# Turning normalised features for the matmuls of a four-layer graph network: 32x32 squares and a trip through DRAM in place of 16-bit DMA transposes

## The chip, the cores and the metric

The kernel runs on one core of one Trainium2 chip. The metric is the time that the device takes for one execution, in microseconds. In the profile the engines are PE (TensorE matmul), PEld (TensorE weight load), DVE (VectorE), ACT (ScalarE), POOL (GpSimd) and SP (SyncE, which here only issues DMAs).

## What is computed

There are 32 independent graphs of 512 nodes with 256 float32 features each, and an integer adjacency matrix per graph (about 3% ones). Four attention layers follow one another; each adds its result to x:

```python
h = relu(layernorm(x))                       # ahead of each of the four layers
# layer 0: att = softmax((h A) h^T / 16 + mask); y = tanh(att (h W0 + b0)); x += tanh(att (y W1 + b1))
# layer 1: Wh = h W^T; e = leaky(src + dst^T) masked; x += softmax(e) Wh
# layer 2: Hh = h W;   e = exp(-leaky(s + d^T)) where adj, else 0; x += elu(e Hh / rowsum)
# layer 3: hl = h W; logits = hl a12 hl^T + Ax^T + Ay; att = softmax(leaky(logits) masked)
#          x += elu(h W_1 + (att h) W_2)
```

Everything is float32. Sizes are fixed: N = 512 nodes are NT = 4 tiles of P = 128, H = 256 features are HC = 2 tiles of 128.

## The kernel before

**One program, planned ahead.** The function `graph(b, ...)` lists the operations of one graph: each `op(engine, cost, after, emit, *keys)` has an engine, a cost in ns, the operations it comes after, and the tiles it uses. The class `Plan` holds all operations of the 32 graphs and of the weights' preparation. `Plan.order` is a list scheduler: each engine takes the ready operation with the earliest due time, if its buffers are free; due times are counted back from deadlines that lie some 32 to 62 us apart per graph (`APART`; the last two graphs use `APART_LAST`). Transfers with a size also queue for a wire of 200 bytes per ns. The result is one fixed order, in which the instructions are issued. Each engine, and the DMA queue of SP, then works in that order and waits where an input is late. The costs (`A_NORM, A_JOIN, V_SPLIT`, `D_TURN` and so on, in ns) thus decide the order, not the time.

**Buffers.** A pool of `PAGES` = 34 pages of 4 KB a partition holds most tiles (x, xn, hT, fa, e, hs, ...); `FLIGHT` = 6 graphs may be under way at once. `planes` (3 buffers) and `planesT` (2) serve the step that the change replaces.

**From x to hT.** `normed(l, xs)` prepares layer l: for each pair g of node tiles, DVE takes the statistics (L557, L558) and adds epsilon (L561), POOL takes the root (L564), DVE forms the offset (L567), and ACT writes the normalised, rectified features `xn` (L571), nodes on partitions. The matmuls need features on partitions, `hT` [128, 2, 512]. [...] per node tile:

1. `split` (L576) copies `xn` into two planes of 16-bit halves, on DVE, or on ACT in layer 1 (`BYACT`);
2. `turn` (L579) is one DMA transpose of the two planes, issued by SP;
3. `join` (L591), on ACT, weaves the planes together into `hT`.

Only layer 0 of graph 0 is turned by PE (`turn_pe` L584, `out_of` L587).

**What uses hT.** `block_sums` forms sums of quarters of `hT` (`hs`, L664 and L667). `seven` multiplies 2x2 blocks with seven products: `by_nodes` (L809) has 128 columns of `hT` or `hs` as the weights and 128 or 129 columns streaming, `features_t` (L783) has a weight matrix as the weights and `hT` streaming, and the scores of layers 0 and 3 (L874, L1040) have both sides from features. `attend` (L758) has a 128x128 block of the attention matrix `e` as the weights and streams the values `v` (257 to 259 columns). `again` (L918) and `second_conv` (L936) are the second half of layer 0. In each case a slice of 128 neighbouring columns, node tile t, is loaded as the weights, for instance

```python
nc.tensor.matmul(T[key][:, : LEAD + H + 1 - lead], e(l, c)[:, t * P : (t + 1) * P],
                 T[f"v{l}"][:, c, lead:], start=(c == 0), stop=(c == NT - 1))
```

Each float32 matmul of the program is two matmul records, with a weight load each, in the profile. A row of scores is made in `leaky_exp_t`: for the first and last two graphs PE turns it (L715), for the others a DVE transpose of 32x32 squares (L719) and two DMAs through DRAM (L723, L728). The adjacency arrives by node tiles (`fetch_adj`, L501), becomes 16-bit codes (L519), and is turned by DMA transposes (L522). Layer 3's maxima take two more DMA transposes a graph (L1072). Outputs leave from POOL (L1154).

Of the kernel before, what the change touches and what calls it, by code (L numbers as in the profile page):

```python
# [13 lines left out]
BF16 = mybir.dt.bfloat16  # L14
U16 = mybir.dt.uint16
AF = mybir.ActivationFunctionType
# [28 lines left out]
A_HALF_BIAS = (345.0, 460.0)  # L45
A_NORM, A_JOIN, V_SPLIT = (491.0, 590.0), (620.0, 767.0), (332.0, 422.0)
D_TURN = (1310.0, 2600.0)
V_SQUARES = (180.0, 270.0)
D_OUT, D_SPREAD = (550.0, 2500.0), (550.0, 4500.0)
D_X, D_ADJ = (550.0, 5000.0), (550.0, 5000.0)  # L50
G_LOAD = (800.0, 5000.0)
# [155 lines left out]
def kernel(  # L207
# [38 lines left out]
    TURNED = 2  # L246
    BYACT = (1,)
    LEAD = 2
# [14 lines left out]
        "w": (pair, F32, "page"), "crest": ([P, 4, N], BF16, "page"),  # L263
        "hs": ([P, 4, N // 2], F32, "page"), "fs": ([P, 4, N // 2], F32, "page"),
        "code": (turned, BF16, "code"), "adj": (turned, I32, "adj"),
        "planes": ([P, 2, H], U16, "planes"), "planesT": ([P, 2 * HC, P], U16, "planesT"),
        "bank": ([P, 512], F32, "bank"), "v": (None, F32, "v"),
# [3 lines left out]
    }  # L271
    POOLS = {"page": PAGES, "v": VALUES, "code": 1, "adj": 1, "planes": 3, "planesT": 2, "bank": 8, "sT": 2,
             "slot": FLIGHT, "ahead": FLIGHT + 1}
# [201 lines left out]
    def graph(b, adj_before, x_before):  # L475
# [12 lines left out]

        def both(kind, l=""):
            return f"{kind}{l}_0", f"{kind}{l}_1"  # L490

# [8 lines left out]
        def fetch_adj(t):  # L500
            nc.sync.dma_start(out=T["adj"][:, t, :], in_=adj[b, t * P : (t + 1) * P, :])  # L501

# [4 lines left out]
        for t in range(NT):  # L507

            got_adj.append(op("D", D_ADJ, got_adj[-1:] if b else [], partial(fetch_adj, t), "adj", size=P * N * 4))
        if b == 0:  # L510
# [41 lines left out]
        def normed(l, xs):  # L552

            def stats(t):
                nc.vector.bn_stats(T[f"st{l}"][:, t, :], T["x"][:, t, :])  # L557
                nc.vector.bn_aggr(T[f"mv{l}"][:, t, :], T[f"st{l}"][:, t, :])  # L558

            def variance(g):  # L560
                nc.vector.tensor_scalar(T[f"ve{l}"][:, two(g)], T[f"mv{l}"][:, two(g), 1], EPS, None, ALU.add)  # L561

            def root(g):
                nc.gpsimd.tensor_tensor(T[f"rstd{l}"][:, two(g)], T[f"ve{l}"][:, two(g)], mhalf[:, two(g)], ALU.pow)  # L564

            def offset(g):
                nc.vector.scalar_tensor_tensor(T[f"off{l}"][:, two(g)], T[f"mv{l}"][:, two(g), 0], -1.0,  # L567
                                               T[f"rstd{l}"][:, two(g)], ALU.mult, ALU.mult)

            def norm(t):  # L570
                nc.scalar.activation(T[f"xn{l}"][:, t, :], T["x"][:, t, :], AF.Relu,  # L571
                                     bias=T[f"off{l}"][:, t : t + 1], scale=T[f"rstd{l}"][:, t : t + 1])

            def split(t):
                bits = T[f"xn{l}"][:, t, :].bitcast(U16).rearrange("p (h b) -> p b h", b=2)
                (nc.scalar.copy if l in BYACT else nc.vector.tensor_copy)(T[f"planes{l}_{t}"], bits)  # L576

            def turn(t):
                nc.sync.dma_start_transpose(out=T[f"planesT{l}_{t}"],  # L579
                                            in_=T[f"planes{l}_{t}"].rearrange("p b h -> p (b h)"))  # L580

            def turn_pe(t, key):
                for c in range(HC):
                    nc.tensor.transpose(T[key][:, c * P : (c + 1) * P], T[f"xn{l}"][:, t, c * P : (c + 1) * P], ident)  # L584

            def out_of(t, key):
                nc.vector.tensor_copy(T[f"hT{l}"][:, :, t * P : (t + 1) * P], T[key][:, : HC * P].rearrange("p (c n) -> p c n", c=HC))  # L587

            def join(t):
                bits = T[f"hT{l}"].bitcast(U16).rearrange("p c (n b) -> p b c n", b=2)  # L590
                nc.scalar.copy(bits[:, :, :, t * P : (t + 1) * P],  # L591
                               T[f"planesT{l}_{t}"].rearrange("p (b c) n -> p b c n", b=2))

            done = []
            for g in range(NT // 2):
                a, d = (op("V", V_STATS, [xs[t]], partial(stats, t), "x", "slot") for t in (2 * g, 2 * g + 1))
                if b == l == 0:
                    for n in ("w0", "att"):
                        ready[n][0]["after"].append(d)
                a = op("V", V_TINY, [a, d], partial(variance, g))  # L600
                r = op("G", G_POW, [a], partial(root, g))
                r = op("V", V_TINY, [r], partial(offset, g))
                for t in (2 * g, 2 * g + 1):
                    flat, over = f"planes{l}_{t}", f"planesT{l}_{t}"
                    a = op("A", A_NORM, [r], partial(norm, t), "x", f"xn{l}")
                    if b == l == 0:

                        key = f"bank_n{t}"
                        a = op("PE", pe(nt=2 * HC), [a], partial(turn_pe, t, key), f"xn{l}", key)
                        done.append(op("V", V_ADD, [a], partial(out_of, t, key), f"hT{l}", key))  # L610
                        continue
                    a = op("A" if l in BYACT else "V", A_JOIN if l in BYACT else V_SPLIT, [a], partial(split, t), f"xn{l}", flat)
                    a = op("D", D_TURN, [a], partial(turn, t), flat, over)
                    done.append(op("A", A_JOIN, [a], partial(join, t), over, f"hT{l}"))
            return done
# [89 lines left out]
        def leaky_exp_t(l, vs, sign):  # L705
# [8 lines left out]
            def turn(t):  # L714
                nc.tensor.transpose(T[key][:, t * P : (t + 1) * P],  # L715
                                    T[v][:, t, 0:1].to_broadcast([P, P]), ident)

            def squares():
                nc.vector.transpose(T[f"sT{l}"].rearrange("p (t j) -> p t j", t=NT), T[v][:, :, 0:32])  # L719

            def collect():
                line.append(dram.tile([N], F32, tag=f"row_{T.places['slot']['number']}", name=f"row{l}_{b}"))
                nc.sync.dma_start(out=line[0].rearrange("(t g j) -> g t j", t=NT, j=32),  # L723
                                  in_=T[f"sT{l}"][0:P:32, :].rearrange("g (t j) -> g t j", t=NT))

# [22 lines left out]
        def attend(l, es, vs, use):  # L748
# [4 lines left out]
            for ts in parts(l):  # L753
                keys = [f"bank_a{l}{t}" for t in ts]

                def product(ts, c, keys):
                    for t, key in zip(ts, keys):
                        nc.tensor.matmul(T[key][:, : LEAD + H + 1 - lead], e(l, c)[:, t * P : (t + 1) * P],  # L758
                                         T[f"v{l}"][:, c, lead:], start=(c == 0), stop=(c == NT - 1))
# [45 lines left out]
        def by_nodes(w, right, x, p, fresh):  # L805

            k = w.shape[2]
            for j in range(2):
                nc.tensor.matmul(p[:, j * k : (j + 1) * k], right(x)[:, j * P : (j + 1) * P], w[:, x - 1, :],  # L809
                                 start=fresh and j == 0, stop=True, skip_group_check=True)  # L810
# [3 lines left out]
        if b == 0:  # L814
# [12 lines left out]
            for t in range(NT):  # L827
                key = f"bank_v0{t}"

                def values(t, key):  # L830
                    for c in range(HC):
                        nc.tensor.matmul(T[key][:, :H], T["hT0"][:, c, t * P : (t + 1) * P], w0_sb()[:, c, :],
                                         start=(c == 0), stop=(c == HC - 1))
# [4 lines left out]
            for c in range(NT):  # L838
                key = f"bank_q0{c}"

                def similar(c, key):
                    for k in range(HC):
                        nc.tensor.matmul(T[key], T["hT0"][:, k, c * P : (c + 1) * P], T["fa0"][:, k, :],
                                         start=(k == 0), stop=(k == HC - 1))
# [6 lines left out]
        else:  # L851
# [20 lines left out]
            def scores0(right, left, x, p, fresh):  # L872
                for j in range(2):
                    nc.tensor.matmul(p[:, j * N // 2 : (j + 1) * N // 2], right(x)[:, j * P : (j + 1) * P], left(x),  # L874
                                     start=fresh and j == 0, stop=True, skip_group_check=True)
# [53 lines left out]
        for g in range(NT // 2):  # L929
            key = f"bank_o{g}"  # L930

            def second_conv(g, key):
                for j in range(2):
                    t = 2 * g + j
                    for k in range(HC):
                        nc.tensor.matmul(T[key][:, j * H : (j + 1) * H], T["zT"][:, k, t * P : (t + 1) * P],  # L936
                                         w1_sb[:, k, :], start=(k == 0), stop=(k == HC - 1))
# [100 lines left out]
        def scores3(x, p, fresh):  # L1038
            for j in range(2):
                nc.tensor.matmul(p[:, j * N // 2 : (j + 1) * N // 2], left(x)[:, j * P : (j + 1) * P], right(x),  # L1040
                                 start=fresh and j == 0, stop=True, skip_group_check=True)
# [159 lines left out]
```

## Time and profile before

| | before |
|---|---|
| median of 3 runs (lowest to highest) | 2353.42 us (2351.95 to 2353.51) |
| profiled execution, first to last instruction | 2353.1 us (its own time is not listed apart) |
| granted TensorE clock | 0.999 |
| records of matmuls, DVE, ACT | 12374, 6060, 3421 |
| DMA packets, moved | 429859, 178.26 MB |
| queue 1 (SP's), share of 16 DMA engines | 31.2% |
| DMA transposes: features, codes, maxima | 508, 124, 64 |

The page gives the busy time of each engine over the whole span, then groups of instructions by line, tile and shape: busy time, mean ns of one, and after the bar the idle time just before them with what ended it. Matmuls overlap, so a mean of 381 ns for one does not mean that they are 381 ns apart; the spacing is read from runs of equal matmuls in the timeline or in the chain. Bytes and packets count the DMA side of each transfer. A wait is put down to what came last.

### The profile page before, as it was taken

The page shows a single profiled execution, that of the slowest core. Times are in us where ns is not written, and L with a number is a line of the kernel's source. Part 1 is how long each engine was busy: PE and PEld are TensorE (multiplying, and loading weights), DVE is VectorE, ACT ScalarE, POOL GpSimd, SP SyncE. Part 2 cuts the span into 40 slices and gives each one's busy share as a digit, 9 for nine tenths or more (in the row PEclk, how much of TensorE's full clock was granted, in tenths as well). Part 3 has the DMA queues.
Part 4 walks back from the last instruction along what each step waited for, and adds up shares of the span by engine and source line. Part 5 has one row for each costly group of instructions (what it writes and reads, how often), then busy time and mean ns, then how long its engine had stood idle before and what let it go on. Part 6 is the DMA issues. An engine that isn't in the chain of part 4 may idle for free.

```text
span 2353.1 us, 37623 instructions
## 1 busy us (share of the span) xinstructions
PE 2328.9 (99%) x12374; PEld 1992.0 (85%) x12374; DVE 2099.7 (89%) x6060; ACT 1719.9 (73%) x3421; POOL 254.2 (11%) x316
## 2 busy tenths in 40 slices
PE   8999999999999999999999999999999999999998
PEld 5789888888888888888898888888888888888887
DVE  8788899989889898898998889989898988987998
ACT  5677778767787677786777877677776778667874
POOL 3000101111011111011110010100101000010110
PEclk9999999999999999999999999999999999999999
DMA  7431233323333332333323334233343333321221
GB/s 192 106 78 28 57 79 79 88 66 83 72 75 84 78 83 66 70 88 90 82 58 74 80 85 90 54 82 70 88 91 68 86 68 73 86 54 33 55 49 42
DMA packets 429859, 178.26 MB, mean 76 GB/s; under 512 B 384128, under 2 KB 401664, under 8 KB 429664
## 3 DMA queue, kind: packets, MB, share of 16 engines
q1 hardware_dynamic: 424288, 157.51, 31.2%
q0 software_dynamic: 5232, 18.23, 2.4%
q8 instruction: 97, 1.59, 0.3%
q14 instruction: 98, 0.80, 0.1%
q10 hardware_dynamic: 144, 0.13, 0.0%
HBM read 67.64 MB, written 16.89 MB: 36 GB/s over the span
## 4 chain that ended last, share of the span: by engine, by line
PE 94%; DVE 4%; DMA 1%; ACT 1%; issue 0%; POOL 0%; DVEq 0%; ACTq 0%
PE bank_a L758 36%; PE bank_z L918 9%; PE bank_s3p L1040 5%; PE bank_o L936 4%; PE bank_q0p L874 4%; PE bank_f3p L783 4%; PE bank_w3p L809 4%; PE bank_v0p L809 4%; PE bank_f0p L783 4%; PE bank_s3q L1040 3%; PE bank_q0q L874 3%; PE bank_v1p L809 2%; PE bank_v3p L809 2%; PE bank_v2p L809 2%; PE bank_v3q L809 2%; PE bank_v1q L809 2%
## 5 line engine op out<-in xcount | busy, mean ns | idle before, releaser
L758 PE MATMUL bank_a<-v,e 128*128 128x258 f32 (+2 forms) x4096 | 1017.7, 381 | 0.9 <-DVE e L956 0.9
L758 PEld LDWEIGHTS bank_a<-v,e 128*128 128x128 f32 x4096 | 744.1, 190 | 108.9 <-issue 18.2
L591 ACT COPY hT<-planesT 128x512 uint16<-128x512 uint16 x508 | 377.8, 769 | 93.9 <-DMA planesT<-planes 93.2
L564 POOL TENSOR_TENSOR rstd<-ve,mhalf 128x2 f32<-128x2 f32 x256 | 216.0, 863 | 1732.3 <-DVE ve L561 1599.4
L571 ACT ACTIVATE xn<-x,off,rstd 128x256 f32<-128x256 f32 x512 | 278.0, 593 | 39.8 <-DVE off L567 38.9
L918 PE MATMUL bank_z<-e,y 128*128 128x512 f32 x512 | 240.8, 593 | 0.0
L557 DVE BATCH_NORM_STATS2 st<-x 128x6 f32<-128x256 f32 x512 | 210.5, 411 | 3.8 <-DMA x<-in_x_dram 3.8
L576 DVE COPY planes<-xn 128x512 uint16<-128x512 uint16 x380 | 156.4, 420 | 17.3 <-DMA planesT<-planes 10.2
L882 ACT ACTIVATE e<-e 128x512 f32<-128x512 f32 x124 | 77.8, 629 | 121.9 <-DVE e L893 61.8
L732 ACT ACTIVATE e<-row,v 128x512 f32<-128x512 f32 x224 | 156.6, 719 | 0.8 <-DMA row<-row 0.7
L735 ACT ACTIVATE e<-e 128x512 f32<-128x512 f32 x256 | 157.1, 630 | 0.0
L918 PEld LDWEIGHTS bank_z<-e,y 128*128 128x128 f32 x512 | 92.7, 190 | 64.9 <-issue 60.5
L695 ACT COPY v<-bank_v1p 128x258 f32<-128x258 f32 x128 | 47.7, 373 | 120.0 <-PE bank_v1p L809 119.3
L936 PE MATMUL bank_o<-w_sb,zT 128*128 128x256 f32 x512 | 118.5, 379 | 0.2 <-ACT zT L922 0.2
L1047 DVE SCALAR_TENSOR_TENSOR e<-bank_s3p,v,mask 128x256 f32<-128x256 f32 x256 | 111.0, 475 | 8.4 <-PE bank_a L758 4.4
L558 DVE BATCH_NORM_AGGREGATE mv<-st 128x2 f32<-128x6 f32 x512 | 93.2, 182 | 17.5
L936 PEld LDWEIGHTS bank_o<-w_sb,zT 128*128 128x128 f32 x512 | 95.8, 190 | 12.8 <-ACT zT L922 0.6
L664 DVE TENSOR_TENSOR hs<-hT,hs 128x256 f32<-128x256 f32 x254 | 105.1, 414 | 1.1
L667 DVE TENSOR_TENSOR hs<-hT 128x512 f32<-128x512 f32 x127 | 86.6, 682 | 14.5 <-ACT hT L591 14.3
L1086 ACT ACTIVATE e<-e,zero 128x512 f32<-128x512 f32 x128 | 88.2, 721 | 12.9 <-DVE crest L1064 11.4
L885 DVE TENSOR_TENSOR e<-bank_q0p,mask 128x512 f32<-128x512 f32 x124 | 84.5, 682 | 13.8 <-PE bank_q0p L874 12.3
L1089 DVE TENSOR_TENSOR e<-e,crest 128x512 f32<-128x512 f32 x128 | 85.9, 682 | 8.3 <-ACT crest L1083 8.1
(202 smaller groups left out, 4891.3 us busy)
## 6 DMA issues: line engine op xcount, KB each, us to landing
adj<-in_adj_dram SPq DMA_DIRECT2D x128, 256.0 KB
x<-in_x_dram SPq DMA_DIRECT2D x31, 512.0 KB
out_dram<-y POOLq DMA_DIRECT2D x31, 512.0 KB, 3.6
row<-row SPq DMA_DIRECT2D x56, 256.0 KB
planesT<-planes SPq DMA_TRANSPOSE x508
codeT<-code SPq DMA_TRANSPOSE x124
crest<-crest SPq DMA_TRANSPOSE x64
row<-sT SPq DMA_DIRECT2D x56, 2.0 KB
```

What stands on the lines that cost most here:

```text
L557: nc.vector.bn_stats(T[f"st{l}"][:, t, :], T["x"][:, t, :])
L564: nc.gpsimd.tensor_tensor(T[f"rstd{l}"][:, two(g)], T[f"ve{l}"][:, two(g)], mhalf[:, two(g)], ALU.pow)
L571: nc.scalar.activation(T[f"xn{l}"][:, t, :], T["x"][:, t, :], AF.Relu, bias=T[f"off{l}"][:, t : t + 1], scale=T[f"rstd{l}"][:, t : t + 1])
L591: nc.scalar.copy(bits[:, :, :, t * P : (t + 1) * P], T[f"planesT{l}_{t}"].rearrange("p (b c) n -> p b c n", b=2))
L735: nc.scalar.activation(e(l, c), e(l, c), AF.Exp, scale=sign)
L758: nc.tensor.matmul(T[key][:, : LEAD + H + 1 - lead], e(l, c)[:, t * P : (t + 1) * P], T[f"v{l}"][:, c, lead:], start=(c == 0), stop=(c == ...
L783: nc.tensor.matmul(p[:, : N // 2], w[:, x - 1, :], right(x), start=fresh, stop=True, skip_group_check=True)
L809: nc.tensor.matmul(p[:, j * k : (j + 1) * k], right(x)[:, j * P : (j + 1) * P], w[:, x - 1, :], start=fresh and j == 0, stop=True, skip_gr ...
L874: nc.tensor.matmul(p[:, j * N // 2 : (j + 1) * N // 2], right(x)[:, j * P : (j + 1) * P], left(x), start=fresh and j == 0, stop=True, skip ...
L918: nc.tensor.matmul(T[f"bank_z{k}"], T["y0"][:, c, k * P : (k + 1) * P], e(0, c), start=(c == 0), stop=(c == NT - 1))
L936: nc.tensor.matmul(T[key][:, j * H : (j + 1) * H], T["zT"][:, k, t * P : (t + 1) * P], w1_sb[:, k, :], start=(k == 0), stop=(k == HC - 1))
L1040: nc.tensor.matmul(p[:, j * N // 2 : (j + 1) * N // 2], left(x)[:, j * P : (j + 1) * P], right(x), start=fresh and j == 0, stop=True, skip ...
```

## The change

The features are turned in pairs of node tiles. `squares(g)` is one DVE transpose of 32x32 squares from `xn` of tiles 2g and 2g+1 (512 elements a partition) into half of a page `xt`. `away(g)` stores that half, 256 KB, to a DRAM tile `sheet`; `back(c)` loads half of `hT` from the sheet, 128 partitions by 8 runs of 64 floats. Both are plain DMAs on SP, two of each a layer; both loads come after both stores. Splits, planes and joins go. The nodes of a pair end up interleaved: column 256 g + 2 p + k of `hT` is node p of tile 2g + k. So wherever a node tile is loaded as weights, the slice takes every second column of a half, by the new helper `nodes`; the adjacency's rows are fetched so that node order agrees along the other axis (two DMAs of 64 rows a tile, into every second partition); and the row of scores is laid out in pairs. The planner has new costs `V_TURN`, `D_HALF` and `D_ROWS`.

```diff
-A_NORM, A_JOIN, V_SPLIT = (491.0, 590.0), (620.0, 767.0), (332.0, 422.0)
+A_NORM, V_TURN = (491.0, 590.0), (600.0, 700.0)
+D_ROWS = (1000.0, 5000.0)
+D_HALF = (550.0, 2500.0)
...
-        "planes": ([P, 2, H], U16, "planes"), "planesT": ([P, 2 * HC, P], U16, "planesT"),
+        "xt": ([P, 2, N], F32, "page"), 
...
+        def nodes(cols, j):
+            return cols[:, j::2]
...
         def fetch_adj(t):
-            nc.sync.dma_start(out=T["adj"][:, t, :], in_=adj[b, t * P : (t + 1) * P, :])
+            for k in range(2):
+                first = t // 2 * 2 * P + k * P + t % 2 * (P // 2)
+                nc.sync.dma_start(out=T["adj"][k::2, t, :], in_=adj[b, first : first + P // 2, :])
...
-            def split(t):
-                bits = T[f"xn{l}"][:, t, :].bitcast(U16).rearrange("p (h b) -> p b h", b=2)
-                (nc.scalar.copy if l in BYACT else nc.vector.tensor_copy)(T[f"planes{l}_{t}"], bits)
-
-            def turn(t):
-                nc.sync.dma_start_transpose(out=T[f"planesT{l}_{t}"],
-                                            in_=T[f"planes{l}_{t}"].rearrange("p b h -> p (b h)"))
+            def squares(g):
+                nc.vector.transpose(
+                    T[f"xt{l}"][:, g, :].rearrange("p (q c n k) -> p k c q n", q=4, c=HC, k=2),
+                    T[f"xn{l}"][:, two(g), :].rearrange("p t (c f q) -> p t c q f", c=HC, q=4))
+
+            def away(g):
+                if not sheet:
+                    sheet.append(dram.tile([2 * P, N], F32, tag=f"sheet_{T.places['slot']['number']}", name=f"sheet{l}_{b}"))
+                nc.sync.dma_start(out=sheet[0][g * P : (g + 1) * P, :], in_=T[f"xt{l}"][:, g, :])
+
+            def back(c):
+                d = sheet[0]
+                nc.sync.dma_start(
+                    out=T[f"hT{l}"][:, c, :].rearrange("p (a r) -> p a r", a=8),
+                    in_=bass.AP(tensor=d.tensor, offset=d.offset + c * (P // 2), ap=[[P, P], [32 * N, 8], [1, P // 2]]))
...
-            def join(t):
-                bits = T[f"hT{l}"].bitcast(U16).rearrange("p c (n b) -> p b c n", b=2)
-                nc.scalar.copy(bits[:, :, :, t * P : (t + 1) * P],
-                               T[f"planesT{l}_{t}"].rearrange("p (b c) n -> p b c n", b=2))
...
-                    a = op("A" if l in BYACT else "V", A_JOIN if l in BYACT else V_SPLIT, [a], partial(split, t), f"xn{l}", flat)
-                    a = op("D", D_TURN, [a], partial(turn, t), flat, over)
-                    done.append(op("A", A_JOIN, [a], partial(join, t), over, f"hT{l}"))
+                    ns.append(a)
+                if ns:
+                    a = op("V", V_TURN, ns, partial(squares, g), f"xn{l}", f"xt{l}")
+                    a = op("D", D_HALF, [a], partial(away, g), f"xt{l}", "slot", size=P * N * 4)
+                    done.append(a)
+            if not b == l == 0:
+                done = [tuple(op("D", D_HALF, done, partial(back, c), f"hT{l}", "slot", size=P * N * 4) for c in range(HC))] * NT
...
-                        nc.tensor.matmul(T[key][:, : LEAD + H + 1 - lead], e(l, c)[:, t * P : (t + 1) * P],
+                        nc.tensor.matmul(T[key][:, : LEAD + H + 1 - lead], nodes(e(l, c)[:, half(t // 2)], t % 2),
...
-                nc.tensor.matmul(p[:, j * k : (j + 1) * k], right(x)[:, j * P : (j + 1) * P], w[:, x - 1, :],
+                nc.tensor.matmul(p[:, j * k : (j + 1) * k], nodes(right(x), j), w[:, x - 1, :],
```

The same replacement of a slice by `nodes` is made in the scores (L874, L1040), in `second_conv` (L936), in graph 0's own products, and in the output of the row turned by PE (L715).

More of the change, by code (lines that the diff above doesn't have):

```diff
@@ L14 @@
 BF16 = mybir.dt.bfloat16
-U16 = mybir.dt.uint16
 AF = mybir.ActivationFunctionType
@@ L246 @@
     TURNED = 2
-    BYACT = (1,)
     LEAD = 2
@@ L263 @@
         "w": (pair, F32, "page"), "crest": ([P, 4, N], BF16, "page"),
-        "hs": ([P, 4, N // 2], F32, "page"), "fs": ([P, 4, N // 2], F32, "page"),
+        "xt": ([P, 2, N], F32, "page"), "hs": ([P, 4, N // 2], F32, "page"), "fs": ([P, 4, N // 2], F32, "page"),
         "code": (turned, BF16, "code"), "adj": (turned, I32, "adj"),
-        "planes": ([P, 2, H], U16, "planes"), "planesT": ([P, 2 * HC, P], U16, "planesT"),
         "bank": ([P, 512], F32, "bank"), "v": (None, F32, "v"),
@@ L271 @@
     }
-    POOLS = {"page": PAGES, "v": VALUES, "code": 1, "adj": 1, "planes": 3, "planesT": 2, "bank": 8, "sT": 2,
+    POOLS = {"page": PAGES, "v": VALUES, "code": 1, "adj": 1, "bank": 8, "sT": 2,
              "slot": FLIGHT, "ahead": FLIGHT + 1}
@@ L487, in half @@
             return slice(i * N // 2, (i + 1) * N // 2)
-        def both(kind, l=""):
-            return f"{kind}{l}_0", f"{kind}{l}_1"
+        def nodes(cols, j):
+            return cols[:, j::2]
         def e(l, c):
@@ L507, in graph @@
         for t in range(NT):
-            got_adj.append(op("D", D_ADJ, got_adj[-1:] if b else [], partial(fetch_adj, t), "adj", size=P * N * 4))
+            got_adj.append(op("D", D_ROWS, got_adj[-1:] if b else [], partial(fetch_adj, t), "adj", size=P * N * 4))
         if b == 0:
@@ L572, in norm @@
                                      bias=T[f"off{l}"][:, t : t + 1], scale=T[f"rstd{l}"][:, t : t + 1])
-            def split(t):
-                bits = T[f"xn{l}"][:, t, :].bitcast(U16).rearrange("p (h b) -> p b h", b=2)
-                (nc.scalar.copy if l in BYACT else nc.vector.tensor_copy)(T[f"planes{l}_{t}"], bits)
-            def turn(t):
-                nc.sync.dma_start_transpose(out=T[f"planesT{l}_{t}"],
-                                            in_=T[f"planes{l}_{t}"].rearrange("p b h -> p (b h)"))
+            def squares(g):
[11 more added lines that the diff above has]
+                    in_=bass.AP(tensor=d.tensor, offset=d.offset + c * (P // 2), ap=[[P, P], [32 * N, 8], [1, P // 2]]))
+            sheet = []
             def turn_pe(t, key):
@@ L586, in out_of @@
             def out_of(t, key):
-                nc.vector.tensor_copy(T[f"hT{l}"][:, :, t * P : (t + 1) * P], T[key][:, : HC * P].rearrange("p (c n) -> p c n", c=HC))
-            def join(t):
-                bits = T[f"hT{l}"].bitcast(U16).rearrange("p c (n b) -> p b c n", b=2)
-                nc.scalar.copy(bits[:, :, :, t * P : (t + 1) * P],
-                               T[f"planesT{l}_{t}"].rearrange("p (b c) n -> p b c n", b=2))
+                nc.vector.tensor_copy(T[f"hT{l}"][:, :, t // 2 * 2 * P + t % 2 : (t // 2 + 1) * 2 * P : 2],
+                                      T[key][:, : HC * P].rearrange("p (c n) -> p c n", c=HC))
             done = []
@@ L602, in normed @@
                 r = op("V", V_TINY, [r], partial(offset, g))
+                ns = []
                 for t in (2 * g, 2 * g + 1):
-                    flat, over = f"planes{l}_{t}", f"planesT{l}_{t}"
                     a = op("A", A_NORM, [r], partial(norm, t), "x", f"xn{l}")
@@ L714, in turn @@
             def turn(t):
-                nc.tensor.transpose(T[key][:, t * P : (t + 1) * P],
+                nc.tensor.transpose(nodes(T[key][:, half(t // 2)], t % 2),
                                     T[v][:, t, 0:1].to_broadcast([P, P]), ident)
             def squares():
-                nc.vector.transpose(T[f"sT{l}"].rearrange("p (t j) -> p t j", t=NT), T[v][:, :, 0:32])
+                nc.vector.transpose(T[f"sT{l}"].rearrange("p (s j k) -> p s k j", s=2, k=2), T[v][:, :, 0:32].rearrange("p (s k) j -> p s k j", k=2))
             def collect():
                 line.append(dram.tile([N], F32, tag=f"row_{T.places['slot']['number']}", name=f"row{l}_{b}"))
-                nc.sync.dma_start(out=line[0].rearrange("(t g j) -> g t j", t=NT, j=32),
-                                  in_=T[f"sT{l}"][0:P:32, :].rearrange("g (t j) -> g t j", t=NT))
+                nc.sync.dma_start(out=line[0].rearrange("(s g j) -> g s j", s=2, j=64),
+                                  in_=T[f"sT{l}"][0:P:32, :].rearrange("g (s j) -> g s j", s=2))
             def spread():
@@ L831, in values @@
                     for c in range(HC):
-                        nc.tensor.matmul(T[key][:, :H], T["hT0"][:, c, t * P : (t + 1) * P], w0_sb()[:, c, :],
+                        nc.tensor.matmul(T[key][:, :H], nodes(T["hT0"][:, c, half(t // 2)], t % 2), w0_sb()[:, c, :],
                                          start=(c == 0), stop=(c == HC - 1))
@@ L842, in similar @@
                     for k in range(HC):
-                        nc.tensor.matmul(T[key], T["hT0"][:, k, c * P : (c + 1) * P], T["fa0"][:, k, :],
+                        nc.tensor.matmul(T[key], nodes(T["hT0"][:, k, half(c // 2)], c % 2), T["fa0"][:, k, :],
                                          start=(k == 0), stop=(k == HC - 1))
@@ L873, in scores0 @@
                 for j in range(2):
-                    nc.tensor.matmul(p[:, j * N // 2 : (j + 1) * N // 2], right(x)[:, j * P : (j + 1) * P], left(x),
+                    nc.tensor.matmul(p[:, j * N // 2 : (j + 1) * N // 2], nodes(right(x), j), left(x),
                                      start=fresh and j == 0, stop=True, skip_group_check=True)
@@ L935, in second_conv @@
                     for k in range(HC):
-                        nc.tensor.matmul(T[key][:, j * H : (j + 1) * H], T["zT"][:, k, t * P : (t + 1) * P],
+                        nc.tensor.matmul(T[key][:, j * H : (j + 1) * H], nodes(T["zT"][:, k, half(t // 2)], t % 2),
                                          w1_sb[:, k, :], start=(k == 0), stop=(k == HC - 1))
@@ L1039, in scores3 @@
             for j in range(2):
-                nc.tensor.matmul(p[:, j * N // 2 : (j + 1) * N // 2], left(x)[:, j * P : (j + 1) * P], right(x),
+                nc.tensor.matmul(p[:, j * N // 2 : (j + 1) * N // 2], nodes(left(x), j), right(x),
                                  start=fresh and j == 0, stop=True, skip_group_check=True)
```

## The prediction

> **What bounds the kernel now.** I read the page first: totals, slices, then the costliest groups.
>
> ```profile
> span 2353.1 us, 37623 instructions
> ...
> PE 2328.9 (99%) x12374; PEld 1992.0 (85%) x12374; DVE 2099.7 (89%) x6060; ACT 1719.9 (73%) x3421; POOL 254.2 (11%) x316
> ...
> PE 94%; DVE 4%; DMA 1%; ACT 1%; issue 0%; POOL 0%; DVEq 0%; ACTq 0%
> ...
> L758 PE MATMUL bank_a<-v,e 128*128 128x258 f32 (+2 forms) x4096 | 1017.7, 381 | 0.9 <-DVE e L956 0.9
> L758 PEld LDWEIGHTS bank_a<-v,e 128*128 128x128 f32 x4096 | 744.1, 190 | 108.9 <-issue 18.2
> L591 ACT COPY hT<-planesT 128x512 uint16<-128x512 uint16 x508 | 377.8, 769 | 93.9 <-DMA planesT<-planes 93.2
> ...
> L576 DVE COPY planes<-xn 128x512 uint16<-128x512 uint16 x380 | 156.4, 420 | 17.3 <-DMA planesT<-planes 10.2
> ```
>
> PE is busy for 2328.9 of 2353.1 us, and the chain that ends last is 94% PE. A busy PE alone need not be a full one, so I looked at the spacing of matmuls in the list of that chain (start, length, what):
>
> ```profile
> 225.00 5.22 PE bank_a L758 x24
> ...
> 386.28 3.45 PE bank_o L936 x16
> ...
> 674.47 3.45 PE bank_o L936 x16
> ```
>
> 24 matmuls of 258 columns in 5.22 us are 217 ns each, 16 of 256 columns 216 ns: steady rates, nothing between them. In the timeline at 1202 us four of 129 columns end 0.61 us after the first starts: less the 0.275 us that one takes, 112 ns each. The same work (L936) recurs at 386.28 and 674.47, four graphs apart: **72.0 us a graph**. The waits of PE then say what is not streaming (us in total, times, longest):
>
> ```profile
> PE bank_n L584 <- ACT xn L571: 8.8, 1, 8.8
> PE bank_f3p L783 <- ACT fa L793: 2.0, 1, 2.0
> PE bank_w3p L809 <- ACT w L1108: 1.9, 1, 1.9
> PE bank_q0p L874 <- DVE e L885: 1.5, 3, 0.6
> ```
>
> 8.8 us is the first load and normalisation of graph 0, which the change leaves alone. The rest sits in the last 250 us or the first 110. From 110 to 2100 us the table by stretches gives PE 1988.36 of 1990. Only about 24 us are idle: 8.8 at the start, 6.5 after the last matmul, 9 in waits. **A gain must come from those 9 us; a loss can come from a slower weight load, from DVE, or from late features.** How near DVE is (PE, PEld, DVE, ACT, POOL in a steady stretch, then in the worst one of the tail):
>
> ```profile
> 1000.00:1100.00 100.00, 100.00 (x535) 85.82 (x534) 91.25 (x270) 72.41 (x147) 12.98 (x15) 1.00 0.35 82
> ```
> ```profile
> 2260.00:2280.00 20.00, 16.06 (x76) 13.57 (x75) 19.15 (x65) 18.64 (x40) 3.14 (x4) 0.91 0.28 53
> ```
>
> At 91% DVE costs PE nothing; in the tail, with DVE at 96% and ACT at 93%, PE loses 3.9 us of 20.
>
> [...]
>
> **The change part by part.** Counts are from the build's order of instructions.
>
> *ACT:* all 508 joins (377.8 us) and 128 splits (75.5 us, 616 ns each) go: 453 us, 73% to 54% of the span. ACT is off the path except for 3.9 us of tail waits (L793, L1108), behind a queue holding joins. I credit half: -2 us.
>
> *DVE:* 380 splits go (-156.4 us); 254 transposes of 512 elements come. Price: L719 took 303 ns for 128; each further element costs (682 - 414)/256 = 1.05 ns by the 512- and 256-element rows, so 303 + 384 x 1.05 = 705 ns. If each element took two such steps: 146 ns fixed (414 - 256 x 1.05) plus 512 x 2.09 = 1218 ns. So +179 to +309 us, net +23 to +153. The net is per graph 5.0 us out and 5.6 (or 9.7) in, against 65.7 of 72: DVE goes to 92% (or 97.8%). I take 705 ns[...]; at 92% PE is the cover, as at 91%: 0 us.
>
> *SP and DMA:* 508 transposes at 1.2 us of SP's time (610 us) become 254 stores and 254 loads, and the adjacency's 128 transfers become 256: 636 more plain issues at about 0.52 us (L728's median) are 331 us, so SP is busy some 280 us less. The features now cross DRAM: 254 x 256 KB are 67 MB out and 67 MB back, the way back in 254 x 1024 = 260,096 pieces, in place of about as many packets of transposes. Queue 1 is 31.2% of the 16 engines; from no change to twice that, it isn't full. What matters is delay: a back load waits for both stores of its layer, and SP holds every x, adjacency, code, crest and row transfer behind that wait, up to 3.6 us (the 512 KB output store's median to landing; I use it for a store). The two back loads I put between 3.6 and 7 us.
>
> *Delay against cover:* from the last attention product of a layer: two reciprocals and adds 1.3, statistics 1.2, root and small steps 1.2, two norms 1.2, square 0.7, store 3.6, back 3.6 to 7, sums (L667) 0.7: 13.5 to 17 us, without queueing. Before: splits, four transposes 1.2 us apart, the last landing 3 to 4.7 us after issue, two joins: 14 to 16. In the new order of PE, priced at the spacings above, 22 to 37 us of other products stand between a layer's last product and the next layer's first of the same graph in most cases, 19 at least (before 22 to 37, 15 at least). So the delay is covered in steady state: 0 us. While the pipeline fills, five graphs' features go out and back in the first 65 us beside x, adjacency and weights (DMA above 0.64 over the first 110 us): I take +2.5 us, bounds 0 to 12.
>
> *PE:* same 12,374 matmuls. Strided weights now feed L758's 4096 loads (217 ns each to hide in), 2276 of 256 columns (216 ns) and 4452 of by_nodes (112 ns, no slack). [...] The 32 turned rows (L715) write PSUM with gaps: 0 to one more 110 ns each, 3.5 us; I take +1.5.
>
> *Sum:* -2 + 0 + 0 + 2.5 + 1.5 = +2 on the profiled span of 2353.1; the median of the runs stands 0.3 above the span. **2355 us.**
>
> **The rivals.**
> *A. Covered (0.45):* as summed; its own range is 2346 to 2363, since the 9 us of waits could go (ACT's relief, down to 2346) or the fill could cost its 12.
> *B. DVE becomes the bound (0.20):* squares near 1.2 us. [...] Against: L719. It decides from about 96% DVE, where the tail window shows PE starving. 70.4 us a graph at that window's 95.8% is 73.5 us, +1.5 x 28 graphs = +42: 2396, between 2360 and 2440.
> *C. Late features (0.20):* back loads over some 10 us, or SP blocked behind them, exceed the 19 to 25 us leads with queueing. For: 256 B pieces, SP in order. Against: DMA at a third, steady leads. 1 us a graph is +31: 2385.
> *D. Weight loads slow down (0.12):* [...]
> *E. ACT's relief empties the tail's waits (0.03 beside A's):* 2346. That DVE and ACT do different work than said is excluded by the order of instructions.
>
> **How the numbers follow.** A gives 0.10 faster, 0.27 within, 0.08 slower; B and C each 0.04 within, 0.16 slower; D slower; E faster: faster 0.13, same 0.35, slower 0.52. (0.2%, 4.7 us, is about what a measurement of this kernel can tell from no change.) The range is 2346 to 2425: it leaves out D, the end of B and some of A's gain, 0.2 in all. The likeliest single case is A.
>
> **What would show it.** Right: PEld rows still 190 ns and by_nodes 112 ns apart; STREAM_TRANSPOSE of 512 near 705 ns; DVE 90%, ACT 54%; PE's waits on hs (L667 of before) below 1 us between 110 and 2100 us; a graph every 72.0 us. Wrong: the squares at 1.2 us with DVE above 95% (B); PE waiting for hs or hT after a DMA (C); L809 rows above 300 ns a matmul[...] (D).

## The result, and the profile after

| | before | after |
|---|---|---|
| median of 4 runs (lowest to highest) | 2353.47 us (2351.95 to 2354.36) | 2391.92 us (2391.5 to 2393.71) |
| ratio, 95% interval | | **1.0164** (1.0149 to 1.0178) |
| profiled execution, first to last instruction | 2353.1 us | 2390.0 us |
| granted TensorE clock | 0.999 | 0.999 |

The change makes the kernel slower by 38.5 us, 1.6%. In the profiled executions it is 36.9 us. The lines of the page after that answer to those of before (totals; the chain that ends last, by engine; the costliest groups; the queue of SP):

```profile
span 2390.0 us, 36965 instructions
...
PE 2360.4 (99%) x12374; PEld 2056.3 (86%) x12374; DVE 2195.4 (92%) x5934; ACT 1351.9 (57%) x2785; POOL 256.0 (11%) x316
...
q1 hardware_dynamic: 450272, 224.07, 35.8%
...
PE 86%; DVE 10%; DMA 2%; issue 1%; ACT 1%; SPq 0%; DVEq 0%; ACTq 0%
...
L770 PEld LDWEIGHTS bank_a<-v,e 128*128 128x128 f32 x4096 | 766.0, 196 | 118.0 <-issue 46.5
...
L577 DVE STREAM_TRANSPOSE xt<-xn 128x512 f32<-128x512 f32 x254 | 280.4, 1111 | 6.1 <-ACT xn L573 6.1
```

Three things stand in these lines. A weight load takes 196 ns where it took 190. A square takes 1111 ns. ACT has fallen from 73 to 57%, and yet the time has risen, since ACT was hardly on the path (1% of the chain before). PE still shows as 99% busy, and that is a trap here: with as many matmuls as before it is "busy" 31.5 us longer, so the loss hides inside busy time. The groups of `by_nodes`, shapes kept apart, show where (after):

```profile
L821 PE MATMUL bank_w3p<-l_w1s,hs 128*128 128x128 f32 x512 | 80.6, 280 | 0.6 <-ACT w L1120 0.6
...
L821 PEld LDWEIGHTS bank_w3p<-l_w1s,hs 128*128 128x128 f32 x512 | 77.0, 196 | 4.9 <-ACT w L1120 1.0
```

and the same two groups before:

```profile
L809 PE MATMUL bank_w3p<-l_w1s,hs 128*128 128x128 f32 x512 | 77.8, 275 | 1.9 <-ACT w L1108 1.9
...
L809 PEld LDWEIGHTS bank_w3p<-l_w1s,hs 128*128 128x128 f32 x512 | 73.6, 191 | 8.0 <-ACT w L1108 2.6 <-DVE w L1112 0.4
```

The load is 5 ns longer, and so is the matmul beside it. The chain that ends last has the same work two graphs apart (start, length, what):

```profile
842.14 3.45 PE bank_o L948 x16
...
987.98 3.45 PE bank_o L948 x16
...
1133.75 3.45 PE bank_o L948 x16
```

That is 145.8 us for two graphs, 72.9 a graph against 72.0. The waits of PE (us in total, times, longest) now end with VectorE's work more often than with ACT's, and none ends with a DMA:

```profile
PE bank_n L596 <- ACT xn L573: 9.1, 1, 9.1
PE bank_f3p L795 <- DVE fa L810: 1.8, 2, 1.0
PE bank_z L930 <- ACT y L921: 1.7, 1, 1.7
PE bank_v1p L821 <- DVE rs L1006: 1.5, 1, 1.5
PE bank_f3p L795 <- DVE hs L676: 1.3, 2, 0.7
```

The steady stretch (length, then PE, PEld, DVE, ACT, POOL, clock, DMA) has DVE at 96.9% where it had 91.3% (over 300 to 2000 us it is 93.5% where it had 90.5%):

```profile
1000.00:1100.00 100.00, 100.00 (x529) 88.69 (x528) 96.93 (x261) 51.96 (x108) 10.98 (x14) 1.00 0.39 104
```

**One more reading, used for every kernel below.** From the start times of all matmul records in the trace I took the time between each matmul and the next, less the time that its own columns take to stream (the steady spacings of before: 429 ns for 512 columns, 217 for 258, 111 for 129, 109.5 for 128, and so on). What is left under 50 ns I call small gaps: PE ran, but the next matmul came a little late. What is 50 ns or more I call big gaps: PE waited. Times in us, one profiled execution each:

| kernel | small gaps | big gaps | big: first 110 us | big: middle | big: last 250 us | span |
|---|---|---|---|---|---|---|
| before | 9.2 | 21.9 | 6.4 | 4.1 | 11.3 | 2353.1 |
| after | 36.3 | 31.9 | 10.3 | 12.7 | 8.9 | 2390.0 |

So the 36.9 us are **27.1 us of small gaps** and 10.0 us of big ones. Of the growth of the small gaps, 22.7 us lie between one of by_nodes' 4452 matmuls and the matmul that follows it, 5.1 ns each: the median spacings went from 110 to 112 ns to 117 to 118 ns.

### The profile page after: what moved, and what is told of

Read it like the earlier page. It is cut to its first block, busy times and chain, and to the rows that moved or that the text cites. A ratio compares the mean times of both kernels' runs of the same rounds, so it can differ in the third digit from the quotient of the medians.

```text
span 2390.0 us, 36965 instructions
## 1 busy us (share of the span) xinstructions
PE 2360.4 (99%) x12374; PEld 2056.3 (86%) x12374; DVE 2195.4 (92%) x5934; ACT 1351.9 (57%) x2785; POOL 256.0 (11%) x316
## 3 DMA queue, kind: packets, MB, share of 16 engines
q1 hardware_dynamic: 450272, 224.07, 35.8%
## 4 chain that ended last, share of the span: by engine, by line
PE 86%; DVE 10%; DMA 2%; issue 1%; ACT 1%; SPq 0%; DVEq 0%; ACTq 0%
PE bank_a L770 32%; PE bank_z L930 9%; PE bank_o L948 4%; PE bank_s3p L1052 4%; PE bank_q0p L886 4%; PE bank_f0p L795 4%; PE bank_f3p L795 4%; PE bank_v0p L821 4%; PE bank_w3p L821 4%; PE bank_q0q L886 3%; PE bank_s3q L1052 3%; PE bank_v3p L821 2%; PE bank_v2p L821 2%; PE bank_v1p L821 2%; PE bank_v1q L821 2%; PE bank_v2q L821 2%
## 5 line engine op out<-in xcount | busy, mean ns | idle before, releaser
L770 PE MATMUL bank_a<-v,e 128*128 128x258 f32 (+2 forms) x4096 | 1046.2, 382 | 2.0 <-ACT e L1104 1.1
L770 PEld LDWEIGHTS bank_a<-v,e 128*128 128x128 f32 x4096 | 766.0, 196 | 118.0 <-issue 46.5
L566 POOL TENSOR_TENSOR rstd<-ve,mhalf 128x2 f32<-128x2 f32 x256 | 220.9, 880 | 1959.5 <-DVE ve L563 1871.4
L577 DVE STREAM_TRANSPOSE xt<-xn 128x512 f32<-128x512 f32 x254 | 280.4, 1111 | 6.1 <-ACT xn L573 6.1
L744 ACT ACTIVATE e<-row,v 128x512 f32<-128x512 f32 x224 | 151.6, 715 | 44.5 <-DMA row<-row 44.5
L747 ACT ACTIVATE e<-e 128x512 f32<-128x512 f32 x256 | 151.5, 625 | 0.1
L968 DVE SCALAR_TENSOR_TENSOR e<-codeT,e 128x512 f32<-128x512 bf16 x128 | 85.2, 684 | 22.6 <-ACT e L747 22.6
L805 ACT ACTIVATE fa<-bank_f3p,l_u 128x256 f32<-128x256 f32 x128 | 60.2, 470 | 65.1 <-PE bank_f3p L795 62.4
L894 ACT ACTIVATE e<-e 128x512 f32<-128x512 f32 x124 | 78.1, 635 | 32.9 <-DVE e L905 26.3
L803 ACT COPY fa<-bank_f0p 128x256 f32<-128x256 f32 x124 | 45.7, 369 | 88.8 <-PE bank_f0p L795 87.4
L952 DVE SCALAR_TENSOR_TENSOR z<-bank_o,rs,b_sb 128x256 f32<-128x256 f32 x128 | 58.3, 479 | 36.3 <-PE bank_o L948 36.1
```

What stands on the lines that cost most here:

```text
L577: nc.vector.transpose(T[f"xt{l}"][:, g, :].rearrange("p (q c n k) -> p k c q n", q=4, c=HC, k=2), T[f"xn{l}"][:, two(g), :].rearrange("p t ...
L744: nc.scalar.activation(e(l, c), row, AF.Prelu, bias=T[v][:, c, HALF + 1 : HALF + 2], alpha=ALPHA)
L770: nc.tensor.matmul(T[key][:, : LEAD + H + 1 - lead], nodes(e(l, c)[:, half(t // 2)], t % 2), T[f"v{l}"][:, c, lead:], start=(c == 0), stop ...
```

## The experiments

Two suspects follow: the weights that are read two floats apart, and the squares that read floats 16 bytes apart. The trip through DRAM is the third. All ratios are to the kernel before, run beside each, with 95% intervals.

**e1: after, weights read as neighbours.**

```diff
-            return cols[:, j::2]
+            return cols[:, j * P : (j + 1) * P]
```

> The changed kernel, but the weights are again 128 neighbouring columns (nodes returns cols[:, j*P:(j+1)*P]); everything else, the order of all instructions included, is as changed. The nodes of the two sides then no longer agree, so the output is not the reference's. Theory W (weight loads of every second column take 196 instead of 190 ns and show only in the 4452 loads of by_nodes): these matmuls go back from 118 to 112 ns apart and the time falls by 4452 x 6 = 27 us, 2392 to about 2365. Theory V (DVE, with squares of 1.11 us, is what PE is late for) or theory L (features land late) as the whole cause: 2388 to 2392, no fall.

Measured: 2379.78 us, 1.0109 (1.0095 to 1.0123), 12.1 us less than after. The groups of by_nodes are back where they were (e1, shapes apart):

```profile
L821 PE MATMUL bank_w3p<-l_w1s,hs 128*128 128x128 f32 x512 | 78.1, 275 | 0.6 <-ACT w L1120 0.6
...
L821 PEld LDWEIGHTS bank_w3p<-l_w1s,hs 128*128 128x128 f32 x512 | 73.9, 191 | 6.1 <-ACT w L1120 1.3
```

The growth of the small gaps is gone: 9.7 us. But the big ones rose from 31.9 to 46.3. A PE that streams faster asks sooner for what VectorE makes, and VectorE, at 97.03 us of the same 100, had little to give (e1, columns as above):

```profile
1000.00:1100.00 100.00, 99.96 (x537) 86.30 (x536) 97.03 (x263) 53.47 (x113) 9.20 (x11) 1.00 0.39 105
```

The time lies between the two forecasts, 2365 and 2388: the weights cost time, and something else was waiting behind them.

**e2 and e3: the kernel before, strided weights alone.** e2 does it in by_nodes only, e3 in attend and, in the same way, in both scores and second_conv.

```diff
-                nc.tensor.matmul(p[:, j * k : (j + 1) * k], right(x)[:, j * P : (j + 1) * P], w[:, x - 1, :],
+                nc.tensor.matmul(p[:, j * k : (j + 1) * k], right(x)[:, j::2], w[:, x - 1, :],
```

> The kernel before, but by_nodes loads every second column of its 256 as weights; everything else is as before, and the output is not the reference's, since the nodes are in another order. Theory W: +24 to +27 us, 2353 to 2377 to 2380, with DVE, ACT and DMA as before. Theories V and L: 2353, as weights cost nothing.

```diff
-                        nc.tensor.matmul(T[key][:, : LEAD + H + 1 - lead], e(l, c)[:, t * P : (t + 1) * P],
+                        nc.tensor.matmul(T[key][:, : LEAD + H + 1 - lead], e(l, c)[:, half(t // 2)][:, t % 2 :: 2],
...
```

> The kernel before, but attend, the scores and second_conv (6372 loads, each with 215 ns of streaming to hide in) load every second column; by_nodes is as before. The output is not the reference's. Theory W: hidden, 2353 to 2357, though these loads show 196 ns too. If 6 ns were lost at every strided load: +38 us, 2391. Theories V and L: 2353.

Measured: e2 2374.79 us, 1.0086 (1.0072 to 1.0100), so 21.4 us more; e3 2357.49 us, 1.0017 (1.0011 to 1.0024), 4.1 us more. The row of by_nodes' loads in e2, then that of attend's loads in e3:

```profile
L809 PEld LDWEIGHTS bank_w3p<-l_w1s,hs 128*128 128x128 f32 x512 | 76.8, 196 | 7.2 <-ACT w L1108 2.6 <-DVE w L1112 0.3
```
```profile
L758 PEld LDWEIGHTS bank_a<-v,e 128*128 128x128 f32 x4096 | 770.8, 196 | 89.8 <-issue 18.2 <-DVE e L956 0.9 <-ACT r L1002 0.3
```

Each load is 6 ns longer in both. Where the matmul beside it streams 128 columns, nearly all of it shows: 22.3 us of small gaps (31.5 against 9.2) over 4452 matmuls are 5.0 ns each. Where it streams 256 or more, e3's 4.1 us of small gaps over 4096 + 2276 matmuls are 0.6 ns each. The load is then nearly hidden. Together 25.5 us, on a kernel whose VectorE had room.

The start times show where the nanoseconds go. In a run of by_nodes' matmuls a load still runs when its own matmul begins: before, it ends 82 ns after that start, in e2 88 ns, and the next load begins 10 ns after that start instead of 2 (medians). So in e2 the lost time follows the matmul whose own weights are strided. After a matmul of by_nodes, one of attend, whose weights are neighbours, comes 7.3 ns late instead of 1.2 (means over 411 such pairs); after one of attend, of 257 to 259 columns, the load of by_nodes ends before its matmul starts (by 26 ns in before, by 19 in after), and the matmul comes 0.8 ns late instead of 0.7.

**e4: after, squares that read neighbours.** The squares take 32 neighbouring floats instead of every fourth. The write keeps its step of 8 bytes.

```diff
-                    T[f"xn{l}"][:, two(g), :].rearrange("p t (c f q) -> p t c q f", c=HC, q=4))
+                    T[f"xn{l}"][:, two(g), :].rearrange("p t (c q f) -> p t c q f", c=HC, q=4))
```

> The changed kernel, but the DVE transposes read 32 neighbouring features instead of every fourth (rearranged as c q f for c f q); weights are loaded as changed. The features come out in another order, so the output is not the reference's. If the 16-byte step of the read is what makes a square of 512 cost 1111 ns, it falls to about 705; if it is the 8-byte step of the write, it stays at 1111. Theory W: with 103 us less DVE work the time falls by at most the 10 us of added waits, to 2382 to 2388. Theory V as the whole cause: to 2355.

Measured: 2376.82 us, 1.0096 (1.0083 to 1.0110), 15.1 us less than after. The group of the squares in e4:

```profile
L577 DVE STREAM_TRANSPOSE xt<-xn 128x512 f32<-128x512 f32 x254 | 176.2, 700 | 6.1 <-ACT xn L573 5.9
```

700 ns: what the prediction took for all. The step of 16 bytes in the read is worth 411 ns of the 1111. The step of 8 bytes in the write costs nothing that can be seen: in e7 below the square writes neighbours too and takes 706 ns. 254 x 411 ns are 104 us less on VectorE, and PE gets 15 of them: its big gaps fall from 31.9 to 17.3, the small ones stay (35.6). That is more than the 10 us that the expectation allowed at most, for it counted only the big gaps that the change had added and not those that were there before.

**e5: both edits, e1 and e4 together.**

> The changed kernel with both edits: weights are 128 neighbouring columns, and the squares read neighbouring features (the output is not the reference's, in node and feature order). Alone they gave -12 and -15 us of the 38. Theory W+V (two causes that partly cover each other: with slower weights DVE's lateness shows less): both together give all of it back, 2350 to 2355. If the parts simply add: 2392 - 27 = 2365. Theory L (a rest from the trip through DRAM): 2360 to 2365 with PE waiting for hs after hT.

Measured: 2352.01 us over 13 runs, 0.9993 (0.9985 to 1.0001). Everything comes back: small gaps 9.2, big 18.2. Alone the two edits gave 12.1 and 15.1 us; together 39.9. **The two causes cover each other.** In e4, where the weights are slow and VectorE has time, the chain has a graph every 72.8 us; in e5, with both mended, every 71.9. In e1, with the loads mended and the squares long, it is 72.6, and with both causes in place no more than 72.9. So a PE slowed to 72.8 leaves VectorE more time for its long squares; with the loads mended alone (e1) it takes that time away again, and VectorE holds PE up instead. Each cause removed alone only uncovers part of the other. The waits of VectorE turn round accordingly (after, then e5; us in total, times, longest):

```profile
DVE z L952 <- PE bank_o L948: 36.1, 20, 3.0
...
DVE hs L679 <- DMA hT<-sheet: 11.0, 15, 2.4
DVE v L711 <- PE bank_v2q L821: 9.4, 12, 2.5
```
```profile
DVE z L952 <- PE bank_o L948: 48.3, 40, 2.9
DVE v L711 <- PE bank_v2q L821: 38.5, 30, 2.5
...
DVE hs L679 <- DMA hT<-sheet: 3.9, 3, 2.9
```

In e5 VectorE waits for PE 40 times instead of 20 in one row and 30 instead of 12 in the other: it has more room. e5 still sends all features to DRAM and back with the same stores and loads, and its ACT is at 58%. So the trip, SP's new order and the freed ACT, taken together, change the time by nothing that the runs can tell from zero.

**e6: after, the planner told the true price of a square.**

```diff
-A_NORM, V_TURN = (491.0, 590.0), (600.0, 700.0)
+A_NORM, V_TURN = (491.0, 590.0), (1020.0, 1111.0)
```

> The changed kernel, with only the planner's price of a square set to what it took: V_TURN (1020, 1111) for (600, 700) ns; the order of the instructions is planned anew. If it is the order, made for squares of 700 ns, that is late: the waits of 32 us fall to about those of the contiguous squares (17), 2377 to 2382. If it is the amount of DVE work: 2388 to 2395, no fall, or worse.

Measured: 2388.83 us, 1.0152 (1.0138 to 1.0166). That is three microseconds of 38, and the two intervals overlap. It is the amount of VectorE's work that costs, as e4 shows by taking it away, and hardly an order built on a wrong price.

**e7, e8, e9: nodes in their natural order.** Can the layout be had without either stride on PE and VectorE? In e7 the nodes are not interleaved: weights, adjacency and the row of scores are as before. `xt` holds the two node tiles apart, a store splits them, and a back load takes 16 runs of 32 floats a partition instead of 8 of 64. The features' step of four moves from the squares' read to the normalisation's read on ACT, which has time (57% busy in after).

```diff
+            def norm_spread(t):
+                nc.scalar.activation(T[f"xn{l}"][:, t, :].rearrange("p (c q f) -> p c q f", c=HC, q=4),
+                                     T["x"][:, t, :].rearrange("p (c f q) -> p c q f", c=HC, q=4), AF.Relu,
...
-                    T[f"xt{l}"][:, g, :].rearrange("p (q c n k) -> p k c q n", q=4, c=HC, k=2),
-                    T[f"xn{l}"][:, two(g), :].rearrange("p t (c f q) -> p t c q f", c=HC, q=4))
+                    T[f"xt{l}"][:, g, :].rearrange("p (k q c n) -> p k c q n", q=4, c=HC, k=2),
+                    T[f"xn{l}"][:, two(g), :].rearrange("p t (c q f) -> p t c q f", c=HC, q=4))
...
-                    in_=bass.AP(tensor=d.tensor, offset=d.offset + c * (P // 2), ap=[[P, P], [32 * N, 8], [1, P // 2]]))
+                    in_=bass.AP(tensor=d.tensor, offset=d.offset + c * 32, ap=[[64, P], [32 * H, 16], [1, 32]]))
```

> A version of the whole: squares and trip through DRAM as in the change, but nodes stay in their natural order (the store splits the two tiles of a pair, the loads fetch 16 runs of 32 floats, 128 B, a partition, so weights and adjacency are as before), and ACT writes xn with the features already spread (it reads x with a step of 16 bytes), so that DVE reads neighbours; V_TURN is 705 in the planner. Theory W+V: PE as before, DVE at 90%, ACT at about 57%, or more if its strided read is slow; 2348 to 2356. Theory L: twice as many pieces in the loads make hT later, PE waits for hs, above 2360.

Measured: 2390.88 us, 1.0158 (1.0144 to 1.0172): no better than after. Small gaps are 9.3 us, so PE's loads are well; big gaps are 60.5. The normalisation's group in after, then in e7, with the squares of e7, and two of PE's waits in e7:

```profile
L573 ACT ACTIVATE xn<-x,off,rstd 128x256 f32<-128x256 f32 x512 | 274.6, 592 | 381.9 <-DVE off L569 380.7
```
```profile
L575 ACT ACTIVATE xn<-x,off,rstd 128x256 f32<-128x256 f32 x508 | 401.8, 851 | 348.2 <-DVE off L567 347.5
...
L580 DVE STREAM_TRANSPOSE xt<-xn 128x512 f32<-128x512 f32 x254 | 179.3, 706 | 37.1 <-ACT xn L575 35.0
```
```profile
PE bank_f3p L796 <- ACT fa L806: 6.2, 7, 3.7
PE bank_w3p L822 <- ACT w L1121: 5.8, 5, 2.2
```

On ACT too the read with a step of 16 bytes is dear: 851 ns where the plain normalisation took 592. PE's longest waits after the start now end with ACT, at 61% of the span. The time is above the 2360 of Theory L, but not for its reason: no wait of PE ends with a DMA. At 73% ACT held PE up less before (2.0 and 1.9 us in these two rows), so its mean is no guide; what makes it late here is not shown.

e8 gives the planner the measured price of this normalisation and a higher one for the back load; e9 keeps e7 but for a plain normalisation.

```diff
-A_NORM, A_SPREAD, V_TURN = (491.0, 590.0), (491.0, 600.0), (612.0, 705.0)
-D_HALF = (550.0, 2500.0)
+A_NORM, A_SPREAD, V_TURN = (491.0, 590.0), (750.0, 851.0), (612.0, 705.0)
+D_HALF, D_BACK = (550.0, 2500.0), (950.0, 3500.0)
```

> The version with natural node order and ACT's spread read, planned with what its parts took: 851 ns for the spread norm (600 before) and 950 ns of SP's time and 3500 ns to landing for a back load (550 and 2500). If its 38 us came from an order made for shorter steps, PE's waits fall from 60 us to about 20: 2350 to 2358. If the spread norm or the 128-byte pieces cost by themselves: 2380 to 2392.

```diff
-                    ns.append(op("A", A_SPREAD, [r], partial(norm_spread, t), "x", f"xn{l}"))
+                    ns.append(op("A", A_NORM, [r], partial(norm, t), "x", f"xn{l}"))
```

> The version with natural node order, but with the plain norm (592 ns) in place of the spread one and the same prices for all else; the squares read neighbours, so features come out in another order and the output is not the reference's. If the mispriced ACT step made it slow: 2350 to 2357. If the loads in 128-byte pieces, with SP held 950 ns for each, did it: 2375 to 2391, with DVE waiting for hT.

Measured: e8 2379.52 us, 1.0111 (1.0097 to 1.0125); e9 2363.10 us, 1.0044 (1.0031 to 1.0058). In orders planned with the old price, the step in ACT's read thus costs 27.8 us (e7 less e9). The plan with dearer prices saves 11.4 (e7 less e8), so here, more than in e6, the prices mattered; e8 changes two of them at once, and which one helped is not shown. e8 stays far from the 2350 to 2358 of an order at fault alone. e9 falls between its two forecasts: without the step most of the loss is gone, but 11.1 us above e5 are left. What differs most from e5 is the finer trip. Its queue of SP, and the wait for features (e9):

```profile
q1 hardware_dynamic: 741280, 224.06, 46.3%
```
```profile
DVE hs L680 <- DMA hT<-sheet: 18.9, 21, 1.9
```

The same bytes in 291,008 more packets take 46.3% of the DMA engines' span instead of 36.0 in e5, a back load holds SP for 967 ns on average against 523 in e5 (single ones vary widely: the medians are 567 and 563, and 952 in e7, whose back loads are those of e9), and VectorE waits for features 21 times instead of 3. That this wait is what PE loses is argued; split store and finer loads were not tried apart, and e9's order was planned with 550 ns of SP's time for a back load. Not tried either: natural order by permuting the weights' rows, so that neither squares nor normalisation need a step. Of the kernels that compute the whole (e6, e7, e8) none beats before; e5 and e9, with nodes or features in another order, only show what single parts cost.

## Why the prediction was right or wrong

The range, 2346 to 2425, holds 2391.9, and slower was the sign most likely. But it holds it because rivals B and C had stretched it to 2425, and that is luck as far as the sum goes: the predicted 2355 is 37 us short, its likeliest case A did not come, and of its signs of being right only the small waits on hs came true. Two terms failed, and both were set at zero.

- **Strided weights, 0 us (PE): failed, in size.** The sum adds nothing for them. That zero was my estimate, and the trace of before has no load of every second column that could show it. Such a load takes 196 ns against 190, and the measurement decides. The mechanism of rival D, weight loads that slow and show first in by_nodes, was right; its size was 5 ns a matmul, 22.7 us in all, and the rows of by_nodes went from 275 to 280 ns, far under D's sign of 300. "4452 of by_nodes (112 ns, no slack)" was the right alarm: 6 ns more on a load put 5 on the spacing. 4452 x 5 ns should have been in the sum's bounds. That these matmuls followed one another 112 ns apart did not show their loads to be free, either: each takes 190 ns and runs 82 ns into its own matmul.
- **"I take 705 ns" (DVE): failed.** It is 1111 ns, near the upper bound of 1218. The arithmetic was sound, for e4's square took 700; what it stood for was not. L719 reads 32 neighbours, the square reads every fourth float, and I let a row with another stride set the price. With 1111 the prediction's own net is 282 - 156 = +126 us on DVE, not +23. Measured: +124 us in these rows, and +95.7 in DVE's total.
- **"It decides from about 96% DVE" (rival B): half right.** DVE became a bound, in stretches of 96.9%, but its mean over 300 to 2000 us is 93.5%: a mean a little over 93 was enough to cost something. B's 2396 is near the 2392 measured by luck, and not for B's reason alone: without the squares' stride the kernel still takes 2376.8 (e4), without the weights' stride 2379.8 (e1). B left PE's own speed as it was; the two costs came together.
- **Delay against cover, 0 us, and rival C: the zero held, C fell.** No wait of PE over 0.2 us ends with a DMA, and e5 costs nothing with the trip in it. The margin is not large: e9's pieces of 128 B, half of the change's 256, put VectorE into 21 waits.
- **The fill, +2.5, and ACT's relief, -2: the signs fit, the sum cannot be told from zero.** In e5's trace the first 110 us have 7.5 us of big gaps against 6.4 before, and the last 250 us 5.8 against 11.3. That is +1.1 and -5.5 in one profile each; e5's interval still includes no change. ACT itself fell to 57%, not 54: the groups' busy times overlap (those of ACT before add up to 1942.6 us, the total says 1719.9), so what a group shows cannot be taken whole from the total. The same holds for DVE's +124 and +95.7.
- **Rows that write PSUM with gaps, +1.5: 0.** The 32 transposes took 273 ns (median) against 272.
- **SP and DMA: as said.** SP's transfers held it for 716 us instead of 1013, some 300 less where 280 were predicted. Queue 1 went from 31.2 to 35.8% of the DMA engines' span, and stores and loads were late for nobody on PE.

## What to carry to other kernels

Read how far apart an instruction's elements lie before borrowing a duration from a row of the same name: here the same operation with the same number of elements took 700 or 1111 ns. Where matmuls of few columns run back to back with a weight load each, nearly every nanosecond on the load can count (here 5 of 6), and it shows in their spacing, not in PE's busy share. When an edit removes one cause and gains less than its size, look for a second that was covered, and remove both before judging either.

## What the runs showed of the hardware

- A weight load of 128 float32 columns two floats apart: 196 ns against 190, about 5 ns of it on the spacing of 128-column matmuls and 0.6 ns on that of 256 columns or more.
- A float32 transpose of 32x32 squares, 512 elements a partition: 700 ns when it reads neighbours and writes 8 bytes apart, 1111 ns when it reads 16 bytes apart, so 0.8 ns more an element. ACT's normalisation of 256 elements: 592 and 851 ns, 1.0 ns more an element. In both the read's step of 16 bytes costs; the square's write step of 8 bytes did not (700 ns with it in e4, 706 without it in e7).
- In a run of 128-column matmuls a load of neighbouring columns ends 82 ns after its own matmul has begun, a strided one 88 ns; with the strided one the next load begins 8 ns later and the next matmul 6 ns later (before, e2).
- Back loads of 256 KB in runs of 128 B held SP 967 ns on average (e9; median 567, and 952 in e7), in runs of 256 B 523 ns (e5; median 563).
